# A segment sum by one-hot products: one-hots made stationary on four column quarters of TensorE, sums placed by a second product

## The chip, the cores and the metric

The kernel runs on one core of a Trainium2 chip. The metric is the device time of one execution in microseconds; for the kernel before, the median of three runs is given. A profile comes from one further execution.

The engines are named as in the profile: PE is TensorE's matmul, PEld its load of the stationary operand, DVE VectorE, ACT ScalarE, POOL GpSimd, SP SyncE, which here issues loads. A matmul has a *stationary* operand, loaded first, and a *moving* one streamed past it; a float32 matmul leaves two records of each in the trace. L239 is line 239 of the kernel; line numbers of the kernel after are its own.

## The reference

One layer of a graph network with 12,500 nodes of 128 features and 412,500 edges of 48. `dst`, the receiving node of each edge, is sorted.

```python
h = jnp.maximum(_layernorm(x, axis=-1), 0.0)
agg = jax.ops.segment_sum(edges, recv, num_segments=N_NODES)   # recv is dst
u = graph_globals[batch]                                        # batch is all 0
z = jnp.concatenate([h, agg, u], axis=1)
out = x + jax.nn.relu(z @ W1 + b1) @ W2 + b2
```

(`edges` is 412,500 x 48, `W1` 240 x 256, `W2` 256 x 128, all float32.) A segment sum adds to each node the rows of its edges. As `dst` is sorted, a run of consecutive edges reaches a narrow span of nodes, 33 edges a node on the average.

## The kernel before, in words

**Edges.** A *chunk* is 768 edges, six (`T`) on each of 128 partitions, 144 KB. Three chunks are a *group* (`GE` = 2304 edges), and two groups a *step* `s`; there are 90 steps. For each sixth of a chunk there is a one-hot matrix of 128 edges by `W` = 32 node places: it compares the number of the place (`iota`) with `rel`, the edge's node less a start (`onehot`, L214, its compare at L218, on DVE, one instruction of 128 x 1152 for a step). `aggregate` (L227, product at L239) makes the edges the stationary operand (128 x 48) and the one-hot the moving one (128 x 32), and the products add up in PSUM as features by nodes: 48 x 80, since the three chunks of a group have their 32 places at 0, 24 and 48 of it. The two groups of a step write to PSUM partitions 0 and 64, so to two column halves of the array, and take turns. `add` (L243) loads the group's place among the nodes into a register of DVE (L246) and adds the 48 x 80 into `aggT` (L251), which holds 48 features of all nodes in SBUF.

The starts come from `dst`: the middle edge of each group gives its place. `load_dst` loads `dst` in parts of up to 126 chunks, with the groups' middles by an extra small load (`md`). `shift_dst` (L174) subtracts, `spread_dst` turns the part through PE (L188) and ACT (L189) into `rel`. `places` (L394) works out all groups' places at once from one load of all middles at the start (`mids`, on ACT's queue). If an edge or a place fell outside what was assumed, a flag (`bad`) would send the kernel into a slow general path behind L566; with these inputs it isn't taken.

**Nodes.** 26 blocks, mostly of 512 nodes: `load_x`, statistics on DVE (`stats`, L266 and L268), `root` on ACT, `factors` on DVE, `normal` on ACT (L296), `plus_b2` on POOL, `turn` (PE, L304) and `keep` (ACT, L310), then the first layer: `first_h` (L325, 512 columns) and `first_a` (L344 and L348, 256 columns each). For its two halves of hidden units, `first_a` uses rows 0 to 47 of the array with `aggT` and rows 64 to 111 with a copy of it that `repeat` (ACT, L332) makes at partition 64. `relu` (ACT, L355), `second` (PE, L363), `result` (DVE, L368) and `store` (POOL, L375) follow.

**Order.** It is written by hand. `todo` lists what each half step does; a step issues the loads for ten groups ahead (`AHEAD`), then two halves of pending work and aggregation, then `add` of the step before and the one-hot two steps ahead. SP issues all loads of edges, `x` and `dst` in that order. 42 buffers hold 42 chunks of edges. `tail_dst` (L407), for the last 84 edges, issues two small loads on SP and works on them on DVE in the same place, 20 steps before the end (L415).

Of the kernel before, what the change touches and what calls it, by code (L numbers as in the profile page):

```python
# [21 lines left out]
def kernel(  # L22
# [22 lines left out]

    T = 6
    CE = P * T
    CG = 3
    GE = CG * CE
    W = 32  # L50
    BEFORE, STEP = 40, 24
    WG = STEP * (CG - 1) + W
    NCH = E // CE
    NGF = NCH // CG
    TAIL = E - NCH * CE
    assert NCH % CG == 0 and TAIL % T == 0 and 0 < TAIL
    TP = TAIL // T
    NG = NGF + 1
# [3 lines left out]
    SPAN = GE * N * PER // E  # L62
    EACH = -(-SPAN // PER)
    NGP = -(-NG // PER) * PER
    HALF = GE * N // (2 * E)
    SLACK = 47

    def centre(g):
        return SPAN * (g // PER) + EACH * (g % PER) + HALF

    def low(g):
        return max(0, min(N - 1, centre(g) - SLACK))

    def high(g):
        return max(0, min(N - 1, centre(g) + SLACK))
# [14 lines left out]

    NS = NG // 2
    assert NG % 2 == 0
    ready = [max(g for g in range(NG) if low(g) - BEFORE < a + m * r) // 2 for a, m, r in blocks]


    parts = [(0, 30)]
    while parts[-1][0] + parts[-1][1] < NCH:
        c0 = parts[-1][0] + parts[-1][1]
        parts.append((c0, min(126, NCH - c0)))
# [4 lines left out]
    aggT = const.tile([DE, N + BEFORE + HI], F32)  # L104
    at_i = const.tile([1, NGP], I32)
    bad = const.tile([1, 1], I32)
    ident = const.tile([P, P], F32)
    iota = const.tile([P, HI], F32)
    ones = const.tile([P, 1], F32)
    eps = const.tile([P, 1], F32)  # L110
    over = const.tile([P, 1], F32)
    w1h = const.tile([D, H], F32)
# [8 lines left out]
    def load_chunk(e, c):  # L121
        nc.sync.dma_start(e, edge_attr[c * CE:(c + 1) * CE].rearrange("(p t) d -> p (t d)", t=T))

# [11 lines left out]
    with fast:  # L135
        ep = fast.enter_context(tc.tile_pool(name="edges", bufs=42))
        ohp = fast.enter_context(tc.tile_pool(name="oh", bufs=4))
# [3 lines left out]
        ps_agg = fast.enter_context(tc.tile_pool(name="ps_agg", bufs=1, space=PSUM))  # L141
# [5 lines left out]
        NACC = 4  # L147
        acc = [ps_agg.tile([P, 512], F32, name=f"ps{i}") for i in range(NACC)]
        NCK = 2 * len(parts) + 2
        chk = one.tile([P, NCK + 1], F32)  # L150
        offrow = one.tile([1, 126], F32)
        off = one.tile([126, 1], F32)
        mids = one.tile([1, NGP], I32)
        cen = one.tile([1, NGP], F32)
        dev = one.tile([1, NGP], F32)
        devc = one.tile([1, NGP], F32)

        edges, onehots, xs, scale, shift, xbs, ht, hids, pos, outs = ({} for _ in range(10))
        banks, dsts, reps = {}, {}, {}

        def load_dst(i, by):
            c0, rows = parts[i]
            di = dp.tile([126, CE], I32, name="di")
            md = dp.tile([126, 1], I32, name="md")
            nc.sync.dma_start(di[:rows], dst[c0 * CE:(c0 + rows) * CE].rearrange("(c e) -> c e", e=CE))
            with nc.allow_non_contiguous_dma(reason="one number a row"):
                by.dma_start(
                    md[:rows],
                    dst[c0 * CE:(c0 + rows) * CE].rearrange("(g e) -> g e", e=GE)[:, GE // 2:GE // 2 + 1]
                    .to_broadcast([rows // CG, CG]))  # L170
            dsts[i] = di, md

        def shift_dst(i):
            c0, rows = parts[i]  # L174
            di, md = dsts[i]
            sub = dp.tile([126, 1], F32, name="sub")
            nc.vector.tensor_tensor(sub[:rows], md[:rows], off[:rows], OP.add)
            df = dp.tile([126, CE], F32, name="df")
            nc.vector.tensor_scalar(df[:rows], di[:rows], sub[:rows], None, OP.subtract)
            dsts[i] = df  # L180

        def spread_dst(i, h):
            c0, rows = parts[i]
            dv = dsts[i].rearrange("c (p t) -> c t p", t=T)
# [8 lines left out]
        def outside(v, n, m, col):  # L193
            sc = mp.tile([P, CE], F32, name="sc")
            nc.scalar.activation(sc[:n, :m], v, AF.Relu, scale=-1.0, accum_out=chk[:n, col:col + 1])
            nc.scalar.activation(sc[:n, :m], v, AF.Relu, bias=over[:n], accum_out=chk[:n, col + 1:col + 2])

        def check_dst(i):
            rows = parts[i][1]
            outside(dsts[i][:rows], rows, CE, 2 * i)  # L200

        def load(g):
            es = []
            for c in range(CG if g < NGF else 1):
                e = ep.tile([P, T * DE], F32, name="e")
                if g < NGF:
                    load_chunk(e, g * CG + c)
                else:
                    load_tail(e)
                es.append(e)  # L210
            edges[g] = es

        def onehot(s):
            oh = ohp.tile([P, 2, CG * T, W], F32, name="oh")  # L214
            n = 2 * CG if 2 * s + 1 < NGF else CG

            def compare(to, k, m, r):
                nc.vector.tensor_tensor(  # L218
                    to, iota[:k, None, :W].to_broadcast([k, m, W]), r[:, :, None].to_broadcast([k, m, W]), OP.is_equal)

            compare(oh.rearrange("p g n w -> p (g n) w")[:, :n * T], P, n * T,
                    rel[:, 2 * s * CG:2 * s * CG + n, :].rearrange("p c t -> p (c t)"))
            if n == CG:
                compare(oh[:TP, 1, :T], TP, T, relt[:TP])
            onehots[s] = oh

        def aggregate(s, part):  # L227
            es, oh, ps = (edges[2 * s], edges[2 * s + 1]), onehots[s], acc[s % NACC]
            if part:
                del edges[2 * s], edges[2 * s + 1], onehots[s]  # L230
            for i in range(part * CG * T // 2, (part + 1) * CG * T // 2):
                c, t = i // T, i % T
                for h in range(2):
                    if 2 * s + h < NGF:
                        k, at, last = P, STEP * c, CG * T
                    else:
                        k, at, last = TP, STEP, T
                    if i < last:
                        nc.tensor.matmul(  # L239
                            ps[HI * h:HI * h + DE, at:at + W], es[h][c][:k, t * DE:(t + 1) * DE], oh[:k, h, i, :],  # L240
                            start=(i == 0), stop=(i == last - 1), skip_group_check=True)

        def add(s):  # L243
            for h in range(2):
                g = 2 * s + h
                _, v = nc.values_load_multi_w_load_instructions(  # L246
                    at_i[0:1, g:g + 1], engines=[DVE], min_val=low(g), max_val=high(g),
                    skip_runtime_bounds_check_because="clamped to these on the chip")
                a, w = (0, WG) if g < NGF else (STEP, W)
                to = aggT[:DE, ds(v[0] + a, w)]  # L250
                nc.vector.tensor_tensor(to, to, acc[s % NACC][HI * h:HI * h + DE, a:a + w], OP.add)  # L251

# [8 lines left out]
        def stats(j):  # L261
            a, m, r = blocks[j]
            st = mp.tile([P, 4, 6], F32, name="st")
            mv = mp.tile([P, 4, 2], F32, name="mv")
# [6 lines left out]
        def root(j):  # L271
            a, m, r = blocks[j]
            st, mv = scale[j]
            sc = mp.tile([P, 4], F32, name="sc4")
# [3 lines left out]
        def factors(j):  # L278
            a, m, r = blocks[j]
            sc, mv = scale[j]  # L280
            sh = mp.tile([P, 4], F32, name="sh4")
# [47 lines left out]
        def repeat(j):  # L329
            a, m, r = blocks[j]  # L330
            rp = mp.tile([P, 4 * P], F32, name="rp")
            nc.scalar.copy(rp[HI:K2, :m * r], aggT[:DE, BEFORE + a:BEFORE + a + m * r])  # L332
            reps[j] = rp


        def first_a(j):
            a, m, r = blocks[j]
            n = m * r
            two = j in reps
            for q in range(0, n, 256):  # L340
                w = min(256, n - q)
                for h in range(NH):
                    if h and two:
                        nc.tensor.matmul(hids[j, h][:, q:q + w], w1a[HI:K2, h * P:(h + 1) * P], reps[j][HI:K2, q:q + w],  # L344
                                         start=False, stop=True, skip_group_check=True)
                    else:
                        c = BEFORE + a + q
                        nc.tensor.matmul(hids[j, h][:, q:q + w], w1a[:DE, h * P:(h + 1) * P], aggT[:DE, c:c + w],  # L348
                                         start=False, stop=True, skip_group_check=True)
# [8 lines left out]
        def second(j):  # L358
            a, m, r = blocks[j]
            pos[j] = ps_o.tile([P, 512], F32, name="po").rearrange("p (r d) -> p r d", r=4)  # L360
            for q in range(r):
                for h in range(NH):
                    nc.tensor.matmul(pos[j][:m, q], hids[j][:, h, q, :m], w2[:, h], start=(h == 0), stop=(h == NH - 1))  # L363

        def result(j):
            a, m, r = blocks[j]
            ot = mp.tile([P, 4, D], F32, name="ot", bufs=3)
            nc.vector.tensor_tensor(ot[:m, :r], pos[j][:m, :r], xbs[j][:m, :r], OP.add)  # L368
# [25 lines left out]
        def places():  # L394
            mf = one.tile([1, NGP], F32)
            nc.vector.tensor_copy(mf, mids)
            nc.vector.tensor_tensor(dev, mf, cen, OP.subtract)
            nc.vector.tensor_scalar(devc, dev, float(-SLACK), float(SLACK), OP.max, OP.min)
# [302 lines left out]
```

## Time and profile before

| What | us |
|---|---|
| Median of 3 runs (389.47 to 390.43) | 389.92 |
| The profiled execution's own time | 390.78 |
| Its span in the trace | 389.0 |
| PE / PEld busy | 333.5 / 272.8 |
| DVE / ACT / POOL busy | 222.1 / 133.8 / 67.0 |
| Mean granted clock of TensorE | 0.947 |
| Bytes moved by DMA, over the span | 95.35 MB, 245 GB/s |

Busy time is a union of intervals. A share of busy time is a mean over stages that may have different limits, so the table says where the engines' time is and not what sets the end; for that, stretches of the span and the waits are looked at. The row of digits of an engine is its busy share in 40 equal slices (9.7 us each), in tenths. In a row of groups stand line, engine, operation, output and inputs with sizes and the count; then the busy time, the mean ns of one, and the idle time ahead of it with what ended it.

### The profile page before, as it was taken

The numbers are of one execution on the slowest core, as the hardware profiler recorded it, in microseconds if no ns is written. First come the engines' busy times: TensorE is split into PE (matmuls) and PEld (weight loads), VectorE is DVE, ScalarE is ACT, GpSimd is POOL, SyncE is SP. The second block draws the span as 40 slices with busy tenths as digits, with TensorE's granted clock in tenths as the row PEclk, the third lists the DMA queues.
The fourth block names the chain that finished last, engine by engine and source line by source line (L and its number), as shares of the span: only waits on it lengthen the run. The fifth ranks groups of instructions, "written<-read, shape, count | busy, mean of one in ns | idle before, by whom it ended". The sixth has DMA issues, their size and how long they took to land. (4 is left out here: it accounts for less than half of the span.)

```text
span 389.0 us, 17383 instructions
## 1 busy us (share of the span) xinstructions
PE 333.5 (86%) x7290; PEld 272.8 (70%) x7291; DVE 222.1 (57%) x576; ACT 133.8 (34%) x268; POOL 67.0 (17%) x92
## 2 busy tenths in 40 slices
PE   3689998899896999899999988799960899799992
PEld 3578886777774877767787776678750687487782
DVE  4465856367456657486557835656601885485610
ACT  3043343245232424164243323264301342245401
POOL 9031221012111121031112111111200301020001
PEclk9999999899999999899999999789985799899987
DMA  6999978998987999998999899998899979990001
GB/s 175 257 272 276 285 226 264 276 282 222 299 268 235 291 288 267 279 303 264 273 278 304 271 275 266 265 302 261 249 295 274 297 217 291 278 276 15 31 0 59
DMA packets 84949, 95.35 MB, mean 245 GB/s; under 512 B 10566, under 2 KB 79688, under 8 KB 84865
## 3 DMA queue, kind: packets, MB, share of 16 engines
q1 hardware_dynamic: 82321, 87.29, 75.7%
q0 software_dynamic: 2304, 6.90, 4.9%
q8 instruction: 58, 0.95, 1.0%
q14 instruction: 26, 0.21, 0.2%
q10 hardware_dynamic: 240, 0.00, 0.0%
HBM read 87.75 MB, written 6.40 MB: 242 GB/s over the span
## 5 line engine op out<-in xcount | busy, mean ns | idle before, releaser
L239 PE MATMUL ps<-oh,e 128*48 128x32 f32 x6456 | 182.3, 214 | 37.6 <-DMA e<-in_edge_attr_dram 19.6
L239 PEld LDWEIGHTS ps<-oh,e 128*48 128x48 f32 x6456 | 168.7, 130 | 59.2 <-DMA e<-in_edge_attr_dram 26.1
L218 DVE TENSOR_TENSOR oh<-iota,rel 128x1152 f32<-128x1152 f32 x90 | 126.0, 1401 | 1.6 <-ACT rel L189 1.6
L251 DVE TENSOR_TENSOR aggT<-aggT,ps 48x80 f32 x180 | 42.1, 234 | 59.4 <-PE ps L239 29.0
L310 ACT COPY hT<-pt 128x512 f32<-128x512 f32 (+2 forms) x26 | 26.4, 1014 | 85.9 <-PE pt L304 85.9
L375 POOL DMA_DIRECT2D out_dram<-ot x27 | 14.8, 550 | 237.9 <-DVE aggT L251 122.1
L325 PE MATMUL ph<-hT,w1h 128*128 128x512 f32 (+2 forms) x104 | 52.6, 634 | 0.0
L363 PE MATMUL po<-w,hid 128*128 128x128 f32 (+1 forms) x392 | 52.0, 287 | 0.7 <-DVE ot L368 0.7
L266 DVE BATCH_NORM_STATS2 st<-xt 128x6 f32<-128x128 f32 (+1 forms) x98 | 21.4, 278 | 54.6 <-DMA xt<-in_x_dram 54.6
L355 ACT ACTIVATE hid<-ph,bias 128x512 f32<-128x512 f32 (+2 forms) x52 | 31.5, 657 | 59.1 <-PE ph L344 40.5
L363 PEld LDWEIGHTS po<-w,hid 128*128 128x128 f32 (+1 forms) x392 | 47.2, 197 | 2.1 <-ACTq L566 0.8
L289 POOL TENSOR_TENSOR xb<-xt,b_sb 128x512 f32<-128x512 f32 (+2 forms) x26 | 32.5, 1256 | 79.0 <-DMA xt<-in_x_dram 78.9
L296 ACT ACTIVATE xn<-xt,sh,sc 128x128 f32<-128x128 f32 (+1 forms) x98 | 40.3, 484 | 3.9 <-PE pt L304 3.0
L348 PEld LDWEIGHTS ph<-aggT,w1a 48*128 48x128 f32 x104 | 17.0, 185 | 20.0 <-issue 13.6
L348 PE MATMUL ph<-aggT,w1a 48*128 48x256 f32 (+1 forms) x104 | 29.9, 404 | 0.0
L325 PEld LDWEIGHTS ph<-hT,w1h 128*128 128x128 f32 x104 | 19.4, 207 | 13.5 <-issue 12.4
L332 ACT COPY rp<-aggT 48x512 f32<-48x512 f32 x23 | 14.2, 617 | 38.1 <-DVE aggT L251 38.0
L344 PE MATMUL ph<-rp,w1a 48*128 48x256 f32 x92 | 25.9, 402 | 0.1
L368 DVE TENSOR_TENSOR ot<-po,xb 128x512 f32<-128x512 f32 (+2 forms) x26 | 17.2, 660 | 3.7 <-issue 1.6
L304 PE MATMUL pt<-ident,xn 128*128 128x128 f32 (+1 forms) x98 | 17.4, 300 | 0.3 <-ACT rel L189 0.3
L344 PEld LDWEIGHTS ph<-rp,w1a 48*128 48x128 f32 x92 | 15.4, 186 | 2.0 <-ACT rp L332 1.7
L189 ACT COPY rel<-pt 128x378 f32<-128x378 f32 (+2 forms) x11 | 7.4, 673 | 22.9 <-PE pt L188 22.9
(71 smaller groups left out, 100.9 us busy)
## 6 DMA issues: line engine op xcount, KB each, us to landing
e<-in_edge_attr_dram SPq DMA_DIRECT2D x537, 144.0 KB, 3.9
xt<-in_x_dram SPq DMA_DIRECT2D x23, 256.0 KB, 4.0
out_dram<-ot POOLq DMA_DIRECT2D x23, 256.0 KB, 4.2
di<-in_dst_dram SPq DMA_DIRECT2D x4, 378.0 KB
xt<-in_x_dram SPq DMA_DIRECT2D x2, 128.0 KB
out_dram<-ot POOLq DMA_DIRECT2D x2, 128.0 KB, 2.2
w1h<-in_L_gnn_W_dram POOLq DMA_DIRECT2D x1, 128.0 KB, 3.0
w<-in_L_gnn_W_dram POOLq DMA_DIRECT2D x1, 128.0 KB, 4.7
```

What stands on the lines that cost most here:

```text
L218: nc.vector.tensor_tensor(to, iota[:k, None, :W].to_broadcast([k, m, W]), r[:, :, None].to_broadcast([k, m, W]), OP.is_equal)
L239: nc.tensor.matmul(ps[HI * h:HI * h + DE, at:at + W], es[h][c][:k, t * DE:(t + 1) * DE], oh[:k, h, i, :], start=(i == 0), stop=(i == last ...
L251: nc.vector.tensor_tensor(to, to, acc[s % NACC][HI * h:HI * h + DE, a:a + w], OP.add)
L266: nc.vector.bn_stats(st[:m, q, :], xs[j][:m, q, :])
L289: nc.gpsimd.tensor_tensor(xb[:m, :r], xs[j][:m, :r], b2_sb[:m, None, :].to_broadcast([m, r, D]), OP.add)
L296: nc.scalar.activation(xn[:m, q], xs[j][:m, q], AF.Relu, bias=shift[j][:m, q:q + 1], scale=scale[j][:m, q:q + 1])
L310: nc.scalar.copy(hT[:, :m * r].rearrange("d (p r) -> d r p", r=r), ht[j][:, :m * r].rearrange("d (r p) -> d r p", r=r))
L325: nc.tensor.matmul(ph, w1h[:, h * P:(h + 1) * P], ht[j][:, :n], start=(h == 0 or not small), stop=False, skip_group_check=True)
L344: nc.tensor.matmul(hids[j, h][:, q:q + w], w1a[HI:K2, h * P:(h + 1) * P], reps[j][HI:K2, q:q + w], start=False, stop=True, skip_group_chec ...
L348: nc.tensor.matmul(hids[j, h][:, q:q + w], w1a[:DE, h * P:(h + 1) * P], aggT[:DE, c:c + w], start=False, stop=True, skip_group_check=True)
L355: nc.scalar.activation(hids[j][:, h, :r, :m], hids.pop((j, h)).rearrange("h (p r) -> h r p", r=r), AF.Relu, bias=bias[:, h:h + 1])
L363: nc.tensor.matmul(pos[j][:m, q], hids[j][:, h, q, :m], w2[:, h], start=(h == 0), stop=(h == NH - 1))
```

## The change

- **Roles swapped.** In `aggregate` the one-hot (128 x 32) is stationary and the edges (128 x 48) are moving. The sums come out as nodes by features. Four chunks share a pass: each has its own 32 PSUM partitions, so its own column quarter, and the four take turns. A step is now 8 chunks (two rounds, `h`, of four), 6144 edges; there are 67 of them and a short one.
- **Centred per chunk.** A chunk's 32 places are centred on its own middle edge, which `shift_dst` takes from `di` itself; the extra loads of middles go. How far each chunk lies from its step's middle is worked out per part by `middles` (some small products and DVE work) into `pos`.
- **Placing.** ACT copies the sums to SBUF (`keep_sums`, twice side by side, features at 0 and 64). DVE compares `iota` with `pos` (`place_columns`, 128 x 2 x 116). Two products a step (`place`) turn the sums and put them at their places: 112 x 218 in PSUM. One `add` a step adds these to `aggT`, which now holds the features twice, at partitions 0 and 64, and `repeat` goes.
- **Loads.** One load brings two chunks (288 KB). 22 buffers of two chunks replace 42 of one. `AHEAD` is 5 steps.
- **Order.** Work is listed by whole steps. `place` and `add` come two steps behind the aggregation (`LAG`) and open the step. `load_tail_dst` is 40 steps before the end and `tail_dst` 20.
- Several memsets at the start move from POOL to DVE.

The core of the diff:

```diff
-    CG = 3
-    GE = CG * CE
     W = 32
-    BEFORE, STEP = 40, 24
-    WG = STEP * (CG - 1) + W
+    CH = P // W
+    CS = 2 * CH
+    ES = CS * CE
+    BEFORE, SECOND, WP = 118, 102, 116
+    WG = SECOND + WP
...
-    aggT = const.tile([DE, N + BEFORE + HI], F32)
+    aggT = const.tile([HI + DE, N + WG], F32)
...
-    def load_chunk(e, c):
-        nc.sync.dma_start(e, edge_attr[c * CE:(c + 1) * CE].rearrange("(p t) d -> p (t d)", t=T))
+    def load_edges(e, c, n):
+        nc.sync.dma_start(
+            e[:, :n], edge_attr[c * CE:(c + n) * CE].rearrange("(c p t) d -> p c (t d)", p=P, t=T))
...
-        ep = fast.enter_context(tc.tile_pool(name="edges", bufs=42))
-        ohp = fast.enter_context(tc.tile_pool(name="oh", bufs=4))
+        ep = fast.enter_context(tc.tile_pool(name="edges", bufs=22))
+        ohp = fast.enter_context(tc.tile_pool(name="oh", bufs=3))
...
-                    nc.tensor.matmul(
-                        ps[HI * h:HI * h + DE, at:at + W], es[h][c][:k, t * DE:(t + 1) * DE], oh[:k, h, i, :],
-                        start=(i == 0), stop=(i == last - 1), skip_group_check=True)
+            for h in range(2) if whole else (1,):
+                for t in range(T):
+                    for q in range(CH) if whole else range(2):
+                        c = CH * h + q if whole else q
+                        k = P if whole or not q else TP
+                        nc.tensor.matmul(
+                            ps[W * q:W * (q + 1), h], oh[:k, c * T + t], es[c][:k, t * DE:(t + 1) * DE],
+                            start=(t == 0 and (h == 0 or not whole)), stop=(t == T - 1), skip_group_check=True)
+
+        def keep_sums(s):
...
+            nc.scalar.copy(to, ps[:k, h, None, :].to_broadcast([k, h.stop - h.start, 2, DE]))
+
+        def place_columns(s):
+            po = ohp.tile([P, 2, WP], F32, name="place")
+            nc.vector.tensor_tensor(po, iota[:, None, :WP].to_broadcast([P, 2, WP]),
+                                    pos[:, s, :, None].to_broadcast([P, 2, WP]), OP.is_equal)
...
+        def place(s):
...
+                nc.tensor.matmul(pp[:HI + DE, SECOND * h:SECOND * h + WP], sums[s % NSB][:k, h, :HI + DE], po[:k, h],
+                                 start=(h == 0 or not whole), stop=(h == 1), skip_group_check=True)
...
-                to = aggT[:DE, ds(v[0] + a, w)]
-                nc.vector.tensor_tensor(to, to, acc[s % NACC][HI * h:HI * h + DE, a:a + w], OP.add)
+            to = aggT[:, ds(v[0] + a, WG - a)]
+            nc.vector.tensor_tensor(to, to, banks_p.pop(s)[:HI + DE, a:WG], OP.add)
...
-                        nc.tensor.matmul(hids[j, h][:, q:q + w], w1a[HI:K2, h * P:(h + 1) * P], reps[j][HI:K2, q:q + w],
-                                         start=False, stop=True, skip_group_check=True)
...
+                    k = slice(0, DE) if n <= 256 else slice(HI * h, HI * h + DE)
+                    nc.tensor.matmul(hids[j, h][:, q:q + w], w1a[k, h * P:(h + 1) * P], aggT[k, c:c + w],
+                                     start=False, stop=True, skip_group_check=True)
...
-            at_half(2 * NS - 40, tail_dst)
+            at(NS - 40, load_tail_dst)
+            at(NS - 20, tail_dst)
...
+            for s in range(max(todo) + 1):
+                if 0 <= s - LAG < NS:
+                    place(s - LAG)
+                    add(s - LAG)
+                if AHEAD <= s + AHEAD - 1 < NS:
+                    load(s + AHEAD - 1)
+                for f, a in todo.get(s, []):
+                    f(*a)
+                if s < NS:
+                    aggregate(s)
+                    keep_sums(s)
                 if 0 < s <= NS:
-                    add(s - 1)
+                    place_columns(s - 1)
                 if s + EARLY < NS:
                     onehot(s + EARLY)
```

The new helper that gives each chunk its place, per part of `dst`:

```python
def middles(i):
    ...
    nc.tensor.matmul(pt[:, :2 * n], same_c[:rows].rearrange("k c w -> k (c w)"), a[:rows, :2 * n],
                     start=True, stop=False, skip_group_check=True)
    nc.tensor.matmul(pt[:, :2 * n], ones[:rows], b[:rows, :n].rearrange("k s h -> k (s h)"),
                     start=False, stop=True, skip_group_check=True)
    ...
    nc.vector.tensor_tensor(pos[:, s0:s0 + n], pt[:, :2 * n].rearrange("p (s h) -> p s h", h=2),
                            wcol[:, None, :].to_broadcast([P, n, 2]), OP.add)
```

436 lines of the change are left out of this document (221 added, 215 removed).

## The prediction, made before the result was known

> **What bounds the kernel now.** I read the page first, its engine totals and its 40 slices.
>
> ```profile
> span 389.0 us, 17383 instructions
> ...
> PE 333.5 (86%) x7290; PEld 272.8 (70%) x7291; DVE 222.1 (57%) x576; ACT 133.8 (34%) x268; POOL 67.0 (17%) x92
> ...
> PE   3689998899896999899999988799960899799992
> ...
> DMA  6999978998987999998999899998899979990001
> GB/s 175 257 272 276 285 226 264 276 282 222 299 268 235 291 288 267 279 303 264 273 278 304 271 275 266 265 302 261 249 295 274 297 217 291 278 276 15 31 0 59
> ...
> L239 PE MATMUL ps<-oh,e 128*48 128x32 f32 x6456 | 182.3, 214 | 37.6 <-DMA e<-in_edge_attr_dram 19.6
> ...
> L218 DVE TENSOR_TENSOR oh<-iota,rel 128x1152 f32<-128x1152 f32 x90 | 126.0, 1401 | 1.6 <-ACT rel L189 1.6
> L251 DVE TENSOR_TENSOR aggT<-aggT,ps 48x80 f32 x180 | 42.1, 234 | 59.4 <-PE ps L239 29.0
> ```
>
> PE looks like the bound at 86%, but the DMA row is as full until slice 36, and empty after it, while PE works on. So there are at least two stages. The table by stretches, cut at the hole in PE's row and at the end of the loads, says more (columns: length, busy time of PE, PEld, DVE, ACT and POOL with counts, granted clock, DMA share, GB/s).
>
> ```profile
> 20.00:288.00 268.00, 248.73 (x5630) 203.42 (x5630) 163.21 (x425) 100.69 (x196) 45.78 (x51) 0.97 0.91 273
> ...
> 283.00:288.00 5.00, 4.92 (x127) 4.47 (x126) 0.00 (x0) 0.00 (x0) 0.00 (x0) 1.00 1.01 336
> 288.00:302.60 14.60, 0.00 (x0) 0.00 (x0) 2.14 (x6) 1.64 (x5) 0.00 (x0) 0.55 0.93 266
> 302.60:350.80 48.20, 44.37 (x971) 35.43 (x972) 34.62 (x89) 16.52 (x34) 9.31 (x11) 0.92 0.89 270
> 350.80:371.50 20.70, 20.34 (x437) 16.06 (x435) 10.93 (x29) 9.19 (x19) 0.56 (x1) 1.00 0.05 17
> ```
>
> The waits name the links (columns: total us, times, longest), and the view of the load's line L122 gives first and last issue and the time to landing.
>
> ```profile
> SPq L122 <- PE ps L239: 62.8, 145, 2.5
> ...
> PEld ps L239 <- DMA e<-in_edge_attr_dram: 26.1, 38, 2.3
> ...
> DVE sub L415 <- DMA md<-in_dst_dram: 18.0, 1, 18.0
> ...
> PE ps L239 <- DVE oh L218: 16.8, 3, 14.7
> ```
> ```profile
> L122 SPq DMA_DIRECT2D e<-in_edge_attr_dram x537: 327/382/2528, 1.3 to 347.0; - x179
> ...
> DMA to landing us min/median/max: 2.2/3.9/5.4
> ```
>
> Until 288 us the loads set the pace: PE waits 38 times for `e` although ten groups are meant to lie ahead, and the DMA engines are 91% busy at 273 GB/s. They are not saturated: for five microseconds they showed 336 GB/s, and SP, which issues every edge load (382 ns each), waits before them in 145 places. Then DVE stands 18.0 us at L415 on a tail number whose load was issued just before it, the one-hots behind it are late, and PE stands 14.7 us. The loads go on, and end at 347.0 + 3.9 = 350.9. From there PE alone sets the end, some 38 us of it, because it still owes the steps it lost.
>
> **The change part by part.** *Aggregation products.* Both kernels issue 3228, two records each (x6456). What does one cost? From the timeline (start, length, line, count):
>
> ```profile
> 286.92 1.00 PE L239 MATMUL ps<-oh,e 128*48 128x32 f32 x36
> ...
> 199.89 1.81 PE L239 MATMUL ps<-oh,e 128*48 128x32 f32 x72
> ...
> 352.99 2.62 PE L239 MATMUL ps<-oh,e 128*48 128x32 f32 x108
> ...
> 355.54 2.05 PE L363 MATMUL po<-w,hid 128*128 128x128 f32 x16
> ...
> 349.79 1.98 PE L325 MATMUL ph<-hT,w1h 128*128 128x512 f32 x4
> ...
> 365.55 0.48 PE L348 MATMUL ph<-aggT,w1a 48*128 48x256 f32 x1
> 365.56 0.48 PE L344 MATMUL ph<-rp,w1a 48*128 48x256 f32 x1
> 365.87 0.38 PE L348 MATMUL ph<-aggT,w1a 48*128 48x256 f32 x1
> 365.88 0.38 PE L344 MATMUL ph<-rp,w1a 48*128 48x256 f32 x1
> ```
>
> 36 more records take 0.81 us: 22.5 ns a record, plus 0.2 us a stretch. Two column halves take turns, so one half gives a record each 45 ns. Wide products cost (1.98 - 0.66) / 3 = 440 ns for 512 columns, 0.86 ns a column, and 2.05 us for 16 of 128 (about 112 ns each, for a load and a stream of 128). At 0.86 ns, 48 columns are 41 ns and 32 are 28: the 45 fits the longer of load (48) and stream (32), not their sum of 69. The change swaps these to a load of 32 and a stream of 48, so the longer is 48 again, 45 ns a quarter. L348 and L344, products in different rows of the array, start 0.01 us apart, and so do their second records 0.3 us later: records of separate tiles run side by side even where each product has two. With four quarters that is 45 / 4 = 11.2 ns a record. Bounds: 11.2 (full overlap of four) and 45 (none); 22.5 would be no gain over now. I take 11.2, to which the pairs are nearest: 6456 x 0.0112 = 72 us, plus 68 stretches x 0.2 = 86 us, for 182.3 now.
>
> The Trainium skill ("TensorE: Matmul & The Clock Gate", on why 56 ns is not 53.3) speaks against this: start to start never falls below about 25 ns, however few columns. Read as a floor for all records together it gives 6456 x 25 = 161 us, no gain. The 22.5 ns measured here lie just under it, so it isn't strictly kept with two tiles; no trace here has four.
>
> *Placing.* 135 products, 270 records of 116 columns at 0.86 ns = 100 ns: 27 us, plus 0.1 us a step of start, 34 us in all, new on PE. *The rest of PE* is 333.5 - 182.3 = 151 us and stays; the few `middles` products cost about 5 at some 0.3 us each. PE busy: 86 + 34 + 156 = 276 us instead of 333.5. While the loads set the pace none of this ends up in the time; it widens the slack and shortens what PE owes after them.
>
> *DVE.* The adds lose 180 x 0.234 = 42 us and come back as 68 of 218 columns. L368 below does 512 columns in 691 ns, so 1.06 ns a column more than L251's 80 in 234: 380 ns, 26 us. One-hots compare as many numbers as before (126 us). `place_columns` is 68 x 232 x 1.22 ns (1401 / 1152) = 19 us. `middles` some 35 small ones at 0.2 = 7. DVE: 222 - 42 + 26 + 19 + 7 = 232 us over the span, about 3.5 us a step.
>
> ```profile
> L332 ACT COPY rp<-aggT 48x512 f32<-48x512 f32 x23 | 14.2, 617 | 38.1 <-DVE aggT L251 38.0
> L368 DVE TENSOR_TENSOR ot<-po,xb 128x512 f32<-128x512 f32 x23 | 15.9, 691 | 0.7
> ```
>
> *ACT* loses the 14.2 us of `repeat` and gains 68 copies of 192 columns: between 617 x 192 / 512 = 0.23 and 0.5 us, I take 0.4, 27 us. That makes 147 us, 2.2 a step, hidden.
>
> *New waits.* `add(s-2)` opens DVE's part of step s and waits for `place(s-2)`, which opens PE's; behind it stand the statistics, `place_columns(s-1)` and `onehot(s+2)`. PE needs that one-hot two steps later, and `place_columns(s-1)` one step later. So DVE is tied to PE's step, but with 3.5 us of work a step and loads that allow 330 / 67 = 4.9, the tie costs nothing; if a step fell under 3.5 us, DVE would be the bound. PE per step is about 276 / 67 = 4.1.
>
> *Loads.* SP issues 270 instead of 537, of two chunks each. One costs 382 ns if the count of instructions decides, 764 if the rows do. Either way a load still waits for the one eight before it (the build's order), which now covers twice the bytes. Five and a half steps of buffers replace seven. After an interruption of SP the engines thus have more queued. I estimate their share at 0.97, between 0.91 (nothing gained) and the 1.01 seen for 5 us. Bytes and packets stay. The load phase, 350.9 - 1.3 = 349.6 us, becomes 349.6 x 0.91 / 0.97 = 328, to end at 329.
>
> *Tail numbers.* Their load moves 20 steps ahead of L415's use: the 18.0 and 14.7 us go. What is late next is the edge load itself. That stall did not delay the loads (266 GB/s in it), so it is paid back only behind 350.9.
>
> *Behind the last load.*
>
> ```profile
> 375.01 1.89 PE L325 MATMUL ph<-hT,w1h 128*128 128x256 f32 x8
> ...
> 377.76 2.03 PE L348 MATMUL ph<-aggT,w1a 48*128 48x256 f32 x8
> ...
> 379.72 1.16 PE L363 MATMUL po<-w,hid 128*128 128x128 f32 x8
> ...
> 381.54 1.13 PE L363 MATMUL po<-w,hid 128*128 128x128 f32 x8 [0.67 <-DVE ot L368]
> ```
> ```profile
> 382.77 0.42 DVE ot L368
> ```
>
> PE then has one whole aggregation (1.3), the last block of 512 (1.98, 1.1, 2.05 for its three products), two turns (0.9), the tail's aggregation (0.3), two placings (0.6 each), an add (0.7), and the closing chain 1.89 + 2.03 + 0.5 + 1.16 + 0.67 + 1.13 + 0.4 = 7.8: together 17.3. From the last sum to the end it is now 389.0 - 383.2 = 5.8. So 23 us behind the load instead of 38.
>
> **Sum.** Span 329 + 23 = 352. The profiled execution took 390.78 for its span of 389.0, 1.8 more, and lies 0.9 above the median of 389.92: 352 + 1.8 - 0.9 = **353 us**.
>
> **Rivals.**
> *The load pace stays* (0.91): if the engines' own packets, or SP at 764 ns and its waits, hold 273 GB/s, the loads end at 351 and the time is 351 + 23 + 0.9 = 375. For it: 0.91 and 0.89 in every long stretch. Against: 336 GB/s in the short one.
> *Quarters overlap only by two*: 22.5 ns, no gain over now: 145 us for the records, and 276 - 72 + 15 = 219 for the rest of PE, its 7.6 before the first product and some 7 of waits at the end: 364. The Trainium skill's floor (same page and section) would make it 219 + 161 = 380. For it: no trace here has four tiles.
> *The loads run at 336 GB/s*: 93 MB take 280 us, PE with 219 + 72 = 291 is then the bound, DVE with 3.5 us a step close behind, near 300.
> *Slower, by PE.* If records in quarters start further apart than (390 - 219) / 6456 = 26.5 ns, aggregation is the bound and the time passes 390; with no overlap (45 ns) it is 219 + 290 = 509. For it: 45 ns is what one tile needs. Against: two tiles do run at 22.5.
>
> **How the numbers follow.** Forecast (343 to 362) 0.58; load pace kept 0.13; overlap by two 0.10; loads at the higher rate 0.07; slower by PE 0.12. The range leaves out the last two: 336 to 380. Faster by over 0.3% (about what a measurement of this kernel tells from no change) takes the first four less a little of the third's upper end: 0.86; within 0.01; slower 0.13.
>
> **What would show it.** Right: 48 aggregation products (96 records) in about 1.3 us; no wait of PE over 3 us for a one-hot late in the span; DMA share of 0.95 or more until about 330; PE waiting for `e` all along; some 23 us behind the last load. Wrong: 96 records in 2.2 us or more; SP's loads at over 0.9 us each; PE waiting for `place` or DVE's add waiting while loads are stopped by full buffers.

## The result, and the profile after

The kernel after took **360.56 us** in the median (358.57 to 363.23, four runs), beside 389.88 (389.47 to 390.43, four runs) for the kernel before: a ratio of 0.9251, 95% interval 0.919 to 0.9313. The profiled execution took 360.19 us, with a span of 358.3. The forecast was 353, its range 336 to 380. Of the runs below, the profiled ones of experiments 2 and 9 and two of the four of experiment 10 lie over 1.5% above the fastest run of their kernel, which is why 10 has no interval.

The totals and the slices (8.96 us each) of the page of the kernel after, with the code queue `q8` and the groups that the prediction priced:

```profile
span 358.3 us, 17287 instructions
...
PE 285.6 (80%) x7584; PEld 222.1 (62%) x7585; DVE 237.6 (66%) x558; ACT 141.1 (39%) x327; POOL 71.6 (20%) x88
...
PE   2377796695899779798898788979879769988792
...
DMA  7999999979698999989999999997899997910001
GB/s 229 322 360 357 340 349 345 315 231 335 175 296 233 339 304 304 366 264 298 288 292 337 324 305 316 311 307 229 258 301 297 314 305 241 317 38 3 31 0 65
...
q8 instruction: 61, 1.00, 1.1%
...
L287 PE MATMUL ps<-e,oh 128*32 128x48 f32 x6456 | 99.0, 215 | 32.3 <-issue 29.6
...
L319 DVE TENSOR_TENSOR aggT<-aggT,pp 112x218 f32 x68 | 25.7, 378 | 97.5 <-PE pp L310 90.7
...
L310 PE MATMUL pp<-place,sums 128*112 128x116 f32 x270 | 48.9, 306 | 8.0 <-issue 4.0
L296 ACT COPY sums<-ps 128x192 f32<-128x192 f32 x68 | 21.6, 317 | 78.7 <-PE ps L287 78.2
...
L300 DVE TENSOR_TENSOR place<-iota,pos 128x232 f32<-128x232 f32 x68 | 28.2, 414 | 0.0
```

PE is busy 48 us less than before (57.5 were forecast), and the time fell by 29. But PE's row is not what the forecast drew: it is ragged from end to end (5 to 8 among the nines), where before it was mostly 8 and 9 outside one hole. DMA moves over 340 GB/s early on, which no long stretch of before did, and its load is over with slice 35. The waits of the kernel after say who holds whom (us in all, times, longest):

```profile
PEld ps L287 <- issue: 39.0, 48, 3.2
...
PE ps L287 <- issue: 29.6, 25, 3.0
...
PE pt L227 <- DVE mid L183: 10.7, 4, 4.4
...
PE pp L310 <- issue: 4.0, 3, 1.9
...
PE ph L393 <- issue: 2.7, 1, 2.7
...
PEld ps L287 <- DMA e<-in_edge_attr_dram: 2.2, 4, 1.2
```
```profile
SPq L124 <- PE ps L287: 113.2, 70, 6.3
...
SPq L124 <- DMA e<-in_edge_attr_dram: 19.0, 44, 1.9
```

The direction has turned. Before, PE waited 19.6 us for edges (`e`); now that wait is next to nothing, and SP stands 113 us in front of its loads until PE gives buffers back (62.8 before). So **PE is the bound**, and it is idle for 358.3 - 285.6 = 72.7 us. Half of that, 29.6 + 4.0 + 2.7 = 36.3 us, ended on "issue": no semaphore that the profile shows held PE. The timeline of PE in the middle of the span shows where:

```profile
196.21 0.53 PE L287 MATMUL ps<-e,oh 128*32 128x48 f32 x27
198.22 0.96 PE L287 MATMUL ps<-e,oh 128*32 128x48 f32 x69 [1.47 <-issue]
...
200.13 0.78 PE L287 MATMUL ps<-e,oh 128*32 128x48 f32 x50
202.41 0.71 PE L287 MATMUL ps<-e,oh 128*32 128x48 f32 x46 [1.50 <-issue]
```

PE breaks off inside one step's aggregation, after 27 of 96 records and after 50 of the next 96, at no boundary of the program. Its operands lie there: the first products of the stretch, from the same tiles, have run. The stretches also give the price of a record: 0.96 - 0.53 = 0.43 us for 42 more is 10.2 ns, beside 22.5 before.

The table by stretches is cut at 314.5 us, where the last edges have landed (columns as in the prediction):

```profile
1.00:314.50 313.50, 253.00 (x7051) 196.94 (x7052) 222.65 (x519) 129.05 (x298) 65.92 (x75) 0.95 0.95 300
314.50:358.30 43.80, 32.58 (x535) 25.20 (x534) 14.77 (x39) 11.79 (x28) 5.46 (x8) 0.86 0.08 27
```
```profile
L124 SPq DMA_DIRECT2D e<-in_edge_attr_dram x269: 367/419/1694, 1.2 to 308.0; - x135
```

A load of two chunks costs SP 419 ns, hardly more than one of a single chunk (382). The loads end at 314.5 and not at 329, and 43.8 us are left behind them and not 23, because with full buffers PE still owes five steps and the short one when the last load is issued.

**What PE waits for** in those breaks is to be seen in the DMA view. Queue `q8` carries instructions: 61 packets of 16 KB here, 58 before. Its bytes follow PE's records: 1.00 MB for 15169 of them here, and 0.44 MB for 6561 in an experiment below, 66 and 67 bytes each. So a packet is some 250 of PE's instructions, and a step, with 192 for its aggregation alone, uses about one. The longest break, in the timeline of PE, and the DMA view of two short windows inside it, 65.90 to 66.55 and 66.55 to 67.60 (share and bytes by queue):

```profile
65.49 0.46 PE L287 MATMUL ps<-e,oh 128*32 128x48 f32 x22
68.96 1.23 PE L287 MATMUL ps<-e,oh 128*32 128x48 f32 x74 [3.02 <-issue]
```
```profile
q1 hardware_dynamic: 190, 0.21, 102.1%
...
q1 hardware_dynamic: 283, 0.32, 97.4%
q8 instruction: 1, 0.02, 5.4%
```

PE stops at 65.95. In the first 0.65 us of the break the DMA engines carry edges and no code. Then one code packet passes (5.4% of 16 engines for 1.05 us, so 0.9 us of one), and about 1.4 us after the window closes PE goes on. All 26 breaks of more than 0.3 us on "issue" look alike in the packet records: PE goes on 1.2 to 1.6 us behind the end of a code packet. And they lie at fixed places in PE's program. The stretches from the end of one break to the end of the next, twice (columns as in the prediction):

```profile
198.22:202.41 4.19, 2.69 (x127) 2.32 (x127) 2.52 (x6) 1.42 (x2) 1.25 (x2) 1.00 0.96 308
202.41:208.63 6.22, 4.93 (x127) 3.11 (x127) 5.52 (x12) 2.42 (x6) 0.59 (x1) 1.00 1.00 336
```

One holds short products and takes 4.2 us, the other long ones as well and takes 6.2, but PE and PEld run 127 and 127 instructions in each. With the semaphore instructions in PE's stream, which the trace holds too, all 26 breaks lie 256 instructions or a multiple of it apart, to within one, and one packet has passed between them for each 256. The same holds for all 121 such breaks in the twelve profiles of this document. So the trace shows that **PE runs out of instructions**: it stops where those of one packet end. The theory to test was why the next packet comes late: **four quarters in turn use instructions twice as fast, and a code packet has to pass among the edge loads.**

### The profile page after: what moved, and what is told of

Same layout as the page of the kernel before. It is cut to its first block, busy times and chain, and to the rows that moved or that the text cites. A ratio compares the mean times of both kernels' runs of the same rounds, so it can differ in the third digit from the quotient of the medians.

```text
span 358.3 us, 17287 instructions
## 1 busy us (share of the span) xinstructions
PE 285.6 (80%) x7584; PEld 222.1 (62%) x7585; DVE 237.6 (66%) x558; ACT 141.1 (39%) x327; POOL 71.6 (20%) x88
## 5 line engine op out<-in xcount | busy, mean ns | idle before, releaser
L259 DVE TENSOR_TENSOR oh<-iota,rel 128x1536 f32<-128x1536 f32 (+1 forms) x70 | 132.9, 1903 | 1.5 <-ACT rel L228 1.5
L287 PE MATMUL ps<-e,oh 128*32 128x48 f32 x6456 | 99.0, 215 | 32.3 <-issue 29.6
L287 PEld LDWEIGHTS ps<-e,oh 128*32 128x32 f32 x6456 | 84.4, 115 | 51.3 <-issue 39.0
L319 DVE TENSOR_TENSOR aggT<-aggT,pp 112x218 f32 x68 | 25.7, 378 | 97.5 <-PE pp L310 90.7
L393 PE MATMUL ph<-hT,w1h 128*128 128x512 f32 (+2 forms) x104 | 53.3, 641 | 3.2 <-issue 2.7
L310 PE MATMUL pp<-place,sums 128*112 128x116 f32 x270 | 48.9, 306 | 8.0 <-issue 4.0
L296 ACT COPY sums<-ps 128x192 f32<-128x192 f32 x68 | 21.6, 317 | 78.7 <-PE ps L287 78.2
L310 PEld LDWEIGHTS pp<-place,sums 128*112 128x112 f32 x270 | 35.2, 192 | 13.9 <-issue 5.4
L357 POOL TENSOR_TENSOR xb<-xt,b_sb 128x512 f32<-128x512 f32 (+2 forms) x26 | 38.9, 1500 | 16.7 <-DMA xt<-in_x_dram 9.9
L393 PEld LDWEIGHTS ph<-hT,w1h 128*128 128x128 f32 x104 | 21.6, 230 | 17.9 <-issue 15.2
L300 DVE TENSOR_TENSOR place<-iota,pos 128x232 f32<-128x232 f32 x68 | 28.2, 414 | 0.0
L334 DVE BATCH_NORM_STATS2 st<-xt 128x6 f32<-128x128 f32 (+1 forms) x98 | 21.3, 276 | 0.0
```

What stands on the lines that cost most here:

```text
L259: nc.vector.tensor_tensor(oh[:k, a:b], iota[:k, None, :W].to_broadcast([k, b - a, W]), r[:, :, None].to_broadcast([k, b - a, W]), OP.is_equal)
L287: nc.tensor.matmul(ps[W * q:W * (q + 1), h], oh[:k, c * T + t], es[c][:k, t * DE:(t + 1) * DE], start=(t == 0 and (h == 0 or not whole)), ...
L300: nc.vector.tensor_tensor(po, iota[:, None, :WP].to_broadcast([P, 2, WP]), pos[:, s, :, None].to_broadcast([P, 2, WP]), OP.is_equal)
L310: nc.tensor.matmul(pp[:HI + DE, SECOND * h:SECOND * h + WP], sums[s % NSB][:k, h, :HI + DE], po[:k, h], start=(h == 0 or not whole), stop= ...
L319: nc.vector.tensor_tensor(to, to, banks_p.pop(s)[:HI + DE, a:WG], OP.add)
L357: nc.gpsimd.tensor_tensor(xb[:m, :r], xs[j][:m, :r], b2_sb[:m, None, :].to_broadcast([m, r, D]), OP.add)
```

## The experiments

Each is given with its ratio to the kernel before, timed beside it. Two rivals ran along: that the loads still set the pace, and that the gain is that of the tail numbers alone.

**1. The kernel before with its tail numbers loaded 20 steps earlier** (the two loads taken out of `tail_dst`), nothing else.

```diff
+            at_half(2 * NS - 80, load_tail_dst)
             at_half(2 * NS - 40, tail_dst)
```

> The kernel before with one part of the change alone: the small loads for the last 84 edges are issued 20 steps ahead of their use. Load pace (the prediction's theory): the stall of 14.7 us goes, the loads still end at about 351 us, and 23 us follow: 375 us. Code supply (PE bound by its work and by waits for its own instructions): PE loses only the stall, 390 - 14.7 = 375 us too; the two part only in the trace, where load pace wants PE to wait for edge loads until the end.

Measured: 371.33 us (368.58 to 374.96), ratio 0.9618 (0.9352 to 0.9883). From its page:

```profile
span 371.2 us, 17382 instructions
...
PE 330.3 (89%) x7290; PEld 270.2 (73%) x7291; DVE 220.8 (59%) x576; ACT 133.8 (36%) x268; POOL 67.8 (18%) x92
...
L239 PE MATMUL ps<-oh,e 128*48 128x32 f32 x6456 | 179.9, 214 | 21.2 <-DMA e<-in_edge_attr_dram 17.4
```

PE still waits 17.4 us for edges: with single loads, the load pace of the prediction holds in this kernel. One moved load gives 389.88 x 0.0382 = 15 us (the interval allows 5 to 25). About half of the change's gain of 29 has nothing to do with how the products are made.

**2. The same with loads of two chunks**, 21 buffers of two in place of 42 of one.

```diff
-                e = ep.tile([P, T * DE], F32, name="e")
...
-                    load_chunk(e, g * CG + c)
...
+                e = ep.tile([P, 2, T * DE], F32, name="e")
...
+                    load_chunks(e, c, 2)
```

> As the run with the earlier tail loads, and the edge loads bring two chunks each (21 buffers of two instead of 42 of one). Load pace: the loads end near 329 or earlier and the time falls by 15 to 22 us, to 353 to 360. Code supply: PE's own work (333.5 us busy, 7.6 before the first product, some 12 at the end) is then the bound, so 365 to 372 us, with SP waiting for buffers.

Measured: 367.33 us (364.04 to 369.69), ratio 0.9542 (0.9358 to 0.9725), as code supply had it. From its page:

```profile
L243 PE MATMUL ps<-oh,e 128*48 128x32 f32 x6456 | 175.6, 214 | 18.9 <-issue 13.1
```

In its profile PE is busy 327.5 us and SP stands 131.2 us in front of full buffers, with the last edges there by 330. By the ratios, the pairs of chunks add 3 us to 1, less than the intervals tell from nothing: PE, busy for 89% of the span, is the bound already. The row shows why the double load gains so little here. PE's wait for edges has shrunk from 17.4 to 3.3 us, and 13.1 us of breaks on "issue" stand in its place (0.8 in experiment 1), at 22.5 ns a record and without quarters. So loads of two chunks bring the breaks by themselves; in the kernel after, which uses instructions faster, there are 29.6 us of them.

**3. The kernel after with one chunk a load.**

```diff
-                    load_edges(e, s * CS + c, 2)
+                    load_edges(e, s * CS + c, 1)
+                    load_edges(e[:, 1:], s * CS + c + 1, 1)
```

> The kernel after with each load of two chunks issued as two loads of one; all else is kept. Load pace: loads end near 351 again and the time is about 375. Code supply: SP had over 100 us of waits for buffers, so most of the extra issuing is hidden: 360 to 367 us.

Measured: 375.57 us (371.25 to 377.44), ratio 0.9739 (0.9352 to 1.0127). Its waits:

```profile
DVE st L335 <- DMA xt<-in_x_dram: 53.4, 19, 4.8
...
PE pp L311 <- DVE place L301: 21.2, 14, 2.8
...
PEld ps L288 <- DMA e<-in_edge_attr_dram: 17.2, 44, 1.3
...
PE ps L288 <- issue: 6.5, 7, 2.2
```
```profile
SPq L124 <- PE ps L288: 13.7, 32, 1.4
```

PE waits for edges again, SP hardly ever for buffers (13.7 us and not 113.2), and the rate is back at some 275 GB/s. The 21.2 us that PE waits for DVE's `place_columns` come from the loads as well: in most of these places DVE has just stood before `stats` (`st`, 53.4 us in all) until a block of `x`, loaded on the same queue, was there. My account of code alone was wrong here (360 to 367 expected): with 537 loads the load path does set the pace. Without the double load the quarters show no gain that the interval tells. And the breaks on "issue" shrink from 29.6 to 6.5 us, with the same products, the same 61 code packets and all of the bytes; PE, which waits for loads here, also gives the code more time.

**4. The kernel after with its products quarter by quarter**, six in a row into each.

```diff
-                for t in range(T):
-                    for q in range(CH) if whole else range(2):
+                for q in range(CH) if whole else range(2):
+                    for t in range(T):
```

> The kernel after with the products ordered quarter by quarter (six of one quarter, then six of the next) instead of in turn; same products, same sums. If the turn of the four quarters is what lets records start 11 to 12 ns apart, one tile's 45 ns returns: 6456 x 0.033 = 215 us more, about 570 us. If the hardware finds the overlap whatever the order: 360 us.

Measured: 430.48 us (428.06 to 431.69), ratio 1.1205 (1.1004 to 1.1406). The timeline, a whole step's 48 products in it and in the kernel after:

```profile
206.43 3.29 PE L287 MATMUL ps<-e,oh 128*32 128x48 f32 x96
```
```profile
310.91 1.23 PE L287 MATMUL ps<-e,oh 128*32 128x48 f32 x96
```

3.29 / 96 = 34 ns a record in a row in one quarter, 1.23 / 96 = 12.8 in turn, starts included. Taking turns is what makes the quarters cheap. The expected 570 us was far off: I had taken 45 ns a record from before, where 48 columns are loaded and 32 streamed; with 32 loaded and 48 streamed it is 34. And the same number of instructions now gives no break of PE over 0.3 us on "issue": spent at 34 ns each, they come in time.

**5. Half the records, each twice as wide**: three products of 96 columns in place of six of 48.

```diff
-                for t in range(T):
+                for t in range(0, T, 2):
...
-                            ps[W * q:W * (q + 1), h], oh[:k, c * T + t], es[c][:k, t * DE:(t + 1) * DE],
+                            ps[W * q:W * (q + 1), h], oh[:k, c * T + t], es[c][:k, t * DE:(t + 2) * DE],
```

> The kernel after with half the aggregation products, each over 96 columns instead of 48: it leaves out the one-hots of every second sixth, and sums columns it then drops. TensorE streams the same number of columns, but has 3228 records and as many weight loads fewer, so about 6,500 instructions less of 15,200. Code supply: PE's unexplained idle time (36 us put down to issue) falls to under 10 and the time to 325 to 338 us. If the idle time belongs to the streaming or to drains: 355 to 361 us.

Measured: 304.97 us (304.28 to 306.14), ratio 0.7895 (0.7837 to 0.7953). Its page, a step in its timeline, and its load phase by stretches:

```profile
span 302.9 us, 10831 instructions
...
PE 265.5 (88%) x4356; PEld 203.2 (67%) x4357; DVE 239.5 (79%) x558; ACT 140.7 (46%) x327; POOL 73.1 (24%) x88
...
q8 instruction: 36, 0.59, 0.8%
...
L287 PE MATMUL ps<-e,oh 128*32 128x96 f32 x3228 | 88.1, 257 | 2.4 <-DVE oh L259 1.5
```
```profile
152.72 1.20 PE L287 MATMUL ps<-e,oh 128*32 128x96 f32 x48
```
```profile
20.00:266.00 246.00, 230.62 (x3968) 177.09 (x3968) 213.63 (x484) 124.08 (x286) 57.90 (x58) 0.97 1.07 357
```

A step's aggregation takes PE as long as before (1.20 for 1.23 us), with half the instructions. The breaks are gone: the idle time before L287 is 2.4 us, 1.5 of it for a one-hot. The time is below the 325 to 338 expected. The span falls by 55.4: 20.1 of PE's busy time and 35.3 of its idle time, about the 36.3 of the breaks. The loads then run through at 357 GB/s.

**6. Two of the six products** in each chunk.

```diff
-                for t in range(T):
+                for t in range(0, T, 3):
```

> The kernel after with only two of six aggregation products of each chunk: two thirds of them are left out. Loads, copies and all other work are kept. Code supply: PE falls by 66 us of work and the waits for instructions, and the loads become the bound: they end near 290 to 300 us and the time is 310 to 325. Load pace as predicted (0.97 of the engines): 345 to 353.

Measured: 296.63 us (295.57 to 297.74), ratio 0.768 (0.7616 to 0.7743). PE is busy 231.4 of 294.0 us, with next to no "issue" in its waits, and the load phase by stretches is as full as in 5:

```profile
20.00:266.00 246.00, 205.48 (x3022) 149.29 (x3014) 219.75 (x503) 122.29 (x295) 61.46 (x61) 0.97 1.07 358
```

Here the loads set the end, at 358 GB/s: 34 us less work on PE than in 5 gave 8 us. That is what these loads take here when PE does not hold them, 64 us under the time of the kernel after and below the 310 to 325 expected. The rival that the loads held the kernel after at its pace (345 to 353 expected) falls.

**7. Half of the edge bytes**, with all of PE's work.

```diff
-                    load_edges(e, s * CS + c, 2)
+                    load_edges(e, s * CS + c, 1)
...
-                es += [e[:, 0], e[:, 1]]
+                es += [e[:, 0], e[:, 0 if s < NSF else 1]]
```

> The kernel after with only the first chunk of each pair loaded and used twice: half of the edges are left out, and the edge bytes halve; PE's work is the same. Code supply, with a fetch time of its own: 355 to 361 us, and the idle time put down to issue stays near 36 us. Code supply held up by the edge loads on the same DMA engines: the idle time falls, 335 to 350. Load pace: far below, under 320 us.

Measured: 319.16 us (317.52 to 322.26), ratio 0.826 (0.8143 to 0.8377). From its page:

```profile
span 318.3 us, 17287 instructions
...
PE 275.4 (87%) x7584; PEld 217.5 (68%) x7585; DVE 238.1 (75%) x558; ACT 141.3 (44%) x327; POOL 74.7 (23%) x88
...
q8 instruction: 61, 1.00, 1.3%
...
L287 PE MATMUL ps<-e,oh 128*32 128x48 f32 x6456 | 97.0, 215 | 8.5 <-issue 6.8
```

The same 61 code packets, the same products, and the idle time before them falls from 32.3 to 8.5 us. So a fetch isn't slow by itself: it is slow among the edge loads of the kernel after. But this run does not show that the bytes did it. Its loads are of one chunk, as in experiment 3, where with all of the bytes 6.5 us on "issue" were left, for 6.8 here. What the two runs have in common is loads of half the size, which land 3.7 and 3.8 us after their issue, for 5.8 in the kernel after. Fewer bytes took more than I expected (335 to 350), 41 us in place of 11 to 26; PE's busy time fell by 10 as well, which I didn't take apart.

**8. The aggregation split**: the step's first round, then `place`, `add` and the load, then its second round.

```diff
             for s in range(max(todo) + 1):
+                if s < NS:
+                    aggregate(s, 0)
                 if 0 <= s - LAG < NS:
                     place(s - LAG)
...
+                if s < NS:
+                    aggregate(s, 1)
                 for f, a in todo.get(s, []):
...
                 if s < NS:
-                    aggregate(s)
                     keep_sums(s)
```

> The kernel after with a step's aggregation cut in two rounds, placing between them and the pending work behind them, so that dense runs of instructions are half as long. Code supply: the waits for instructions fall from 36 to some 15 us, and a second stretch a step costs about 0.3 us x 67 = 20: 355 to 365 us. Otherwise only the cost: 375 to 385 us.

Measured: 352.27 us (348.65 to 355.14), ratio 0.9063 (0.8936 to 0.919). Its waits:

```profile
PEld ps L293 <- issue: 39.0, 77, 2.1
...
PE ps L293 <- issue: 21.3, 22, 1.9
```

The breaks shrink from 29.6 to 21.3 us (some 15 were expected), and by the ratios the time is 7 us under that of the kernel after (0.9063 and 0.9251), though the two intervals touch. It beats the kernel before; a gain over the kernel after isn't shown.

**9. The split, with two repairs at its end.**

```diff
-            for s, f, j in ((h - 3, turn, x1), (h - 3, keep, x1), (h - 3, turn, x2), (h - 3, keep, x2),
+            for s, f, j in ((h - 4, turn, x1), (h - 4, keep, x1), (h - 3, turn, x2), (h - 3, keep, x2),
...
-                for t in range(T):
-                    for q in range(CH) if whole else range(2):
+                for t, q in ([(t, q) for t in range(T) for q in range(CH)] if whole
+                             else [(t, q) for q in range(2) for t in range(T)]):
```

> The split kernel with two changes at its end: block x1 is turned a step before x2, and the last, short aggregation does its six full products and then its six of 14 rows, in place of taking turns. Both theories agree: the 2.01 us wait for ACT's copy goes, and the 24 records of 2.47 us take about 0.8, so some 3.5 us less than the split kernel: a span of about 347, 349 us (346 to 351). If the time does not move, what ends last is not PE's chain.

Measured: 349.56 us (349.19 to 355.85), ratio 0.9116 (0.9047 to 0.9186); against 8, no difference that the intervals tell. The next run has the same repairs and shows where they went.

**10. The same, the second round halved once more**, half of the pending work between the halves.

```diff
+                    aggregate(s, 1, 0)
+                    for f, a in jobs[:len(jobs) // 2]:
+                        f(*a)
+                    aggregate(s, 1, 1)
```

> The same, with the second round of a step's aggregation halved again, and half of the pending work between the halves. Code supply: what counts is how many instructions PE runs through in a short time, so PE's issue waits (21 us in the split kernel) fall to some 10 to 15, and the time is 338 to 345 us. Rival, that the split gained by something else (buffers freed earlier, an earlier placing): 347 to 351, as without it, with the same 21 us of issue waits, or a little more for two more starts of a stretch a step.

Measured: 351.76 us in the median of four (348.53, 349.17, 354.34 and 359.18; the profiled one took 349.17). Its timeline near the end:

```profile
324.03 1.32 PE L294 MATMUL ps<-e,oh 128*32 128x48 f32 x24
...
330.06 0.71 PE L379 MATMUL pt<-ident,xn 128*128 128x128 f32 x2 [1.73 <-ACT xn L371]
```

The wait of 2.01 us for ACT's copy (`hT`) has become one of 1.73 for ACT's `normal` (`xn`), and the short aggregation, 2.47 us for 24 records in 8, still takes 1.32. The finer split leaves 16.8 us of "issue" breaks before the products, between the two expectations, and no shorter time. So the time favours the rival: what 8 gained isn't simply the length of a run of products, or half a step is short enough already. The runs don't tell these apart.

## Why the prediction was right in its number, and where it was wrong

- **What bounds the kernel before**: right in its parts. Experiment 1 bears out the stall of the tail number, and 3 that single loads hold the pace at some 275 GB/s.
- **Aggregation at 11.2 ns a record**: right in size. 10.2 ns by the stretches above, and 1.23 us for the stretch priced at 1.28. Its working was in part lucky: it divided 45 ns a quarter by four, but a quarter in a row takes 34 ns (experiment 4), and four in turn come at 10.2 and not at 34 / 4 = 8.5. The group's 99.0 us, for 86, hold stretches broken in two, which start anew, and slow ones near the end (2.02 us for 96 records where the granted clock was 0.56). The floor of the Trainium skill ("TensorE: Matmul & The Clock Gate", on why 56 ns is not 53.3), which would have made it an estimated 161 us, doesn't hold over four column tiles together: the measurement decides. In one quarter alone, 34 ns lie above it.
- **The rest of PE**: for all of PE's busy time 276 us forecast, 285.6 measured. Placing was mis-sized, 34 us for 48.9, as a step's four records take 0.65 us. The other products came out at 285.6 - 99.0 - 48.9 = 138 for 156, which made up for it.
- **DVE and ACT**: 232 forecast for 237.6, and 147 for 141.1. `place_columns` was too low (0.28 for 0.414 us), the add right (380 for 378 ns), the copies a little high (0.4 for 0.317). None of them sets the end.
- **The tail stall goes**: right, and worth some 15 us (experiment 1). "What is late next is the edge load itself" was wrong; PE's own instructions are late next.
- **Loads**: this is **the step that failed**. I let the edge loads go on setting the pace, raised their share from 0.91 to 0.97, and kept "PE waiting for `e` all along". In the runs, a load of two chunks costs SP what one of a single chunk does (419 and 382 ns), the rate reaches 357 GB/s when nothing holds it (experiments 5 and 6), and in the kernel after the loads are held up by full buffers, 113 us of them, while DVE's add waits for `place` (90.7 us): the prediction's own sign of being wrong. A share of 0.91 went with 273 GB/s and one of 1.07 with 357, so bytes didn't go by the share alone either (273 / 0.91 = 300, 357 / 1.07 = 334). The Trainium skill ("Perfetto Trace Analysis", Engine Utilization and its Roofline) puts 100% at 358 GB/s and says that a core alone can go beyond; here experiments 5 and 6 stay at 357 and 358.
- **Behind the last load**: 23 us forecast, 43.8 measured. It follows from the same step: if PE is the bound, the buffers are full at the end.
- **The sum** was 329 + 23 = 352 for the span; it is 314.5 + 43.8 = 358.3. An error of 14.5 and one of 21 went against each other. The number was right by luck; the chain in it was not.
- **The rivals**: the unchanged load pace came true where loads stay single (375.57 us for its 375). That of the higher load rate had the mechanism, PE as the bound, but its "near 300" allowed PE only some 7 us of waits behind its first product; the 36 us of breaks stand in no part of the prediction. Nothing in the trace of before named them: with its single loads, 0.7 us of "issue" stood before its products.

**What is shown and what is argued.** Shown: PE breaks off where the 256 instructions of a code packet end, and goes on 1.2 to 1.6 us behind the next packet. The breaks go when PE needs fewer instructions (experiment 5) or uses them more slowly (4); they shrink to a quarter with loads of one chunk (3 and 7); and loads of two chunks bring them to the kernel before too (2). The packet records also show the delay: a code packet starts, in the median, 2.5 us after PE has begun the 256 instructions in front of it, 1.8 in experiment 3 and 1.1 in 7. With 1.0 us of passing and some 1.4 behind it that is 4.9 us, and the first of the two stretches above kept PE busy for only 2.7. Argued: that PE asks for code as it begins a block, and that the request waits in line. The trace shows when a packet passes but not when it was asked for, and the runs don't tell whether the size of a load, the bytes on their way at once or their rate delays it.

## What to carry to other kernels

When a PE stage is made of many short products, count its instructions a microsecond beside its busy time: idle time that ends on "issue" in the middle of a stretch, with a code packet just before its end and the same number of instructions between one break and the next, says that products should get wider or fewer, not cheaper. Larger loads can bring it on. When a change makes an engine and a transfer faster at once, work out both bounds anew, the sum of the engine's work and the transfer at its highest rate, before deciding which one paces. And split a gain by undoing parts: here about half came from one load issued earlier.

## What the hardware did that I had not expected

- **Code over the DMA engines.** 16 KB a packet, 256 of PE's instructions, about 1.0 us in passing, and PE goes on 1.2 to 1.6 us behind it. 36 us of breaks at 192 instructions in 1.23 us among 300 GB/s of two-chunk loads; 6.5 before the products with one-chunk loads at 275 GB/s; none to speak of at half the instructions, or at 34 ns a record.
- **One quarter alone** takes 34 ns a record (32 loaded, 48 streamed), four in turn 10.2 to 12.8; 96 columns cost four in turn the same 1.20 us for half the records.
- **A load of two chunks** (256 rows of 1152 bytes) takes SP 419 ns for the 382 of a single one, and lifts the rate from 273 to as much as 357 GB/s.
- **Products of 14 rows and of 128 in turn**: the last 24 records, half of them on 14 rows, took 2.47 us in experiment 8, where the two kinds alternate, and 1.32 in 10, where twelve of each follow one another. The granted clock was 1.00 in both, so the few rows aren't slow in themselves; changing between the kinds is.
